# A decoder layer on one core: the context's values of four heads in one run of matmuls, with changes to loads, stores and the last norm

## The chip, the core and the metric

The kernel runs on one core of a Trainium2 chip. The core has a matmul engine (TensorE, PE in the profile; PEld is its loading of the stationary operand), VectorE (DVE), ScalarE (ACT), GpSimd (POOL), and SyncE (SP), which here only issues DMAs. Matmuls write to PSUM, eight banks of 512 fp32 columns for 128 partitions; the other operands lie in SBUF. Each engine works through its own queue in order, and semaphores tie the queues together. The metric is the device time of one execution in microseconds.

## The reference

One decoder layer with three sublayers, each followed by a residual sum and a layer norm. `x` has 8 sequences of 100 tokens and 1024 features, the context 8 sequences of 722 tokens.

```python
# 1: gated retention, 8 heads (128 for q and k, 256 for v)
o = rms(((rope(x@Wq)*scale) @ rope(x@Wk).T * D) @ (x@Wv)) * silu(x@Wg);  x = layernorm(x + o@Wo)
# 2: attention over the context and the own tokens: 16 query heads, 4 key/value heads of 128
q, k, v = rope(rms_norm(x@wq)), rope(rms_norm(x@wk)), x@wv
k = concat([rms_norm(ctx@wk_ctx), k]);  v = concat([ctx@wv_ctx, v])     # 722 + 100 rows, per sequence
x = layernorm(x + softmax(q@k.T*scale + mask) @ v @ wo)                 # each k/v head serves 4 query heads
# 3: feed-forward, 1024 -> 4096 -> 1024
x = layernorm(x + (silu(x@w_gate.T) * (x@w_up.T)) @ w_down.T)
```

## The kernel before

Activations lie features first: [128, 8 blocks, 400 tokens], in two halves of four sequences (`N` = 400). Every large product is made of three matmuls: an operand is split into a high part (a cast to fp32r on ACT) and a low part (the rest, a subtraction on DVE), and `mm3` adds high x high, high x low and low x high into one PSUM bank (L90, L93, L94; with them all products share these three lines). `split` and `split2` (L63 to L68) make the parts.

The order of the stages is retention with its output projection (`out_proj`, L238), the projections of queries, own keys and own values ("l2", L729), the attention loop (L773), the second output projection, the feed-forward, and the last norm (`norm_last`, L1099). `x` after a norm goes to DRAM (`zd`, `zd2`) and comes back in `out_proj` as `rs` (L264), two buffers, to be added as residual.

The context's weights: `core(h)` of the retention (L538) also splits one of the eight blocks of `wc` for each head (keys and values of the four heads in turn) and stores it to `wcd` (L561 to L566): SP stores the high part and its negative, and a DMA of GpSimd adds the raw weight to the latter, so that the low part is left. It is loaded ready-made later by `load_ws`, into tag `w`, which has four buffers of 1 MB.

The attention loop goes over 8 sequences ("batches", `b`) and 4 key/value heads (`kv`). For each batch, `load_context` brings the context in two parts of 362 and 360 tokens (`SH`, `SN`), in eight loads of two feature blocks each, and splits it into `cz`: the four buffers of the pool `big`, so only one batch's context is there. For each head:

- `context_keys` (L693): two projections of 24 matmuls (weights stationary, 362 or 360 context columns moving) into PSUM tag "a" (three banks); squares and a sum over partitions on POOL (L706), keys to `kall` (two buffers); the sums go by DRAM (`row`, then `rr`) from a row into columns and become the scale `rk` (L798 to L809). The first two heads of batch 0 are made during "l2" (`early`).
- `context_values` (L713): the same with the values' weights; the result, features first, is copied to `cvt`, turned by six transposes on PE (L794) into tokens first, and split into `vall` (two tiles, used in turn; seven chunks of 128 tokens by 128 features, the last ones partly own tokens loaded from `vd`).
- scores (L817): seven chunks, each 3 matmuls of 400 columns (four query heads x 100 tokens; 216 for the chunk of own tokens only), into tag "s" (four banks), evicted to `s` (one buffer) by DVE (L824) and ACT (L828); running maximum on DVE (L829), its reduction over partitions on POOL; subtraction, exponential, split into `ph` and `pl`, sum (L836 to L851).
- the products with `vall` (L854 to L859) in the order of chunks 5, 6, 0, 1, 2, 3, 4, into the one bank of tag "v"; the quotient, and the store to `o2d`.

The order of instructions on each engine is not written by hand: a planner takes the program and its own costs, and at each point puts next what is ready and stands first in program order; a buffer goes to whichever tile is written next. Work for later heads therefore runs ahead as far as buffers allow. `pin` and `issue_after` fix the order in a few places, and `pin`ned in `norm_last` are the subtractions `less(i)`, each over a pair of feature blocks.

Memory of pools is stacked: `y2` (the second output projection's `y` and `rs`, opened before the attention's pools, L764) has its own place beside them, and a tile of a later pool can lie where a tile of a closed pool lay and then waits for its last use.

Of the kernel before, what the change touches and what calls it, by code (L numbers as in the profile page):

```python
# [8 lines left out]
F32 = mybir.dt.float32  # L9
# [7 lines left out]
P = 128  # L17
# [5 lines left out]
SC, SH = 722, 362  # L23
# [17 lines left out]
def decoder_layer(ctx, tc, xT, cT, w1, wo1, w2, wo2, wc, w3, wd, gw, qw, kw, trig, dec, mask, out):  # L41
# [15 lines left out]
    def f32(ap):  # L57
        return ap.bitcast(F32)
# [23 lines left out]
    def load_ws(i):  # L82
        w = wp.tile([P, 2, KT * P], FR, tag="w", name="w", bufs=4)
        nc.sync.dma_start(out=f32(w), in_=f32(wcd[i]))
        return w
# [91 lines left out]
    wcd = dr.tile([2 * NKV, P, 2, KT * P], FR, name="wcd")  # L177
# [60 lines left out]
    def out_proj(half, w, load_o, res, yp, ybufs, p, make_z, dst, z, steps={}):  # L238
# [7 lines left out]
        for ms in [range(first)] + [[m] for m in range(first, KT)]:  # L246
# [15 lines left out]
            for m, acc in zip(ms, accs):  # L262
                rs = yp.tile([P, N], F32, tag="rs", name="rs", bufs=2)
                nc.sync.dma_start(out=rs, in_=res[half, :, m])  # L264
# [63 lines left out]
    def scaled(y, r, dst, z=None, behind=None):  # L328
        cast = None
        for m in range(KT):  # L330
# [6 lines left out]
            nc.sync.dma_start(out=dst(m), in_=y[:, m])  # L337
# [139 lines left out]
    with sbuf("l1", 2) as p:  # L477
# [60 lines left out]
        def core(h):  # L538
# [26 lines left out]
            nc.sync.dma_start(out=f32(wcd[h]), in_=f32(w))  # L565
            nc.gpsimd.dma_start(out=f32(wcd[h])[:, 1], in_=st, accum_op=ALU.add)  # L566
# [126 lines left out]
    def context_keys(kv):  # L693

        kall = ka.tile([P, 2, SC + T], FR, tag="kall", name="kall")
        wk = load_ws(2 * kv)
# [16 lines left out]
    def context_values(kv):  # L713

        wv = load_ws(2 * kv + 1)
        vt = ka.tile([P, SC], F32, bufs=1, tag="cvt", name="cvt")
        for hf in range(2):
            copy = nc.scalar.copy if hf == 0 else nc.vector.tensor_copy
            copy(vt[:, hf * SH:hf * SH + SN[hf]], proj(wv, cz[hf], SN[hf]))
        return vt  # L720
# [5 lines left out]
    for kv in range(NKV):  # L726
        groups += [[(kv, i) for i in range(2)], [(kv, i) for i in range(2, 5)]]
# [36 lines left out]
    y2pool = sbuf("y2", 1)  # L764
    y2p = y2pool.__enter__()
    with sbuf("cx", 2) as p, sbuf("c1", 1) as p1:

        ph = p1.tile([P, NC, N], FR, name="ph")
        pl = p1.tile([P, NC, N], FR, name="pl")
        valls = [p1.tile([P, NC, 2, P], FR, name=f"vall{i}") for i in range(2)]  # L770
        for t in [ph[:, 0], pl[:, 0]] + [v[:, 6] for v in valls]:
            nc.gpsimd.memset(f32(t), 0.0)
        for b in range(B):  # L773
            if b > 0:
                load_context(b)
            for kv in range(NKV):
                if early:
                    kall, row = early.pop(0)
                else:
                    step, (kall, row) = context_keys(kv)  # L780
# [3 lines left out]
                vall = valls[kv % 2]  # L784
                nc.sync.dma_start(out=f32(vall[C5:P, 5]), in_=f32(vd[kv, 0:P - C5, b]))
                nc.sync.dma_start(out=f32(vall[0:R6, 6]), in_=f32(vd[kv, P - C5:T, b]))
# [3 lines left out]
                vt = context_values(kv)  # L790
# [476 lines left out]
```

## Time and profile before

| | us |
|---|---|
| median of 3 runs (2482.09 to 2486.21) | 2483.2 |
| the profiled execution's own time | 2485.66 |
| its span in the profile | 2483.9 |
| PE busy | 2459.2 |
| DVE busy | 1953.3 |
| ACT busy | 1340.1 |
| POOL busy | 460.2 |
| from 920 to 1600 us (attention): DVE, ACT, POOL busy of 680 | 622.6, 414.7, 254.8 |

A page line such as "PE 2459.2 (99%) x14068" is busy time, share of the span and count of instructions. The slices cut the span into 40 equal parts of 62 us; a digit is the busy share in tenths. In the windows view each line has a stretch, its length, then busy time and count for PE, PEld, DVE, ACT and POOL, the granted TensorE clock, the share of DMA and GB/s. In the timeline a line has start, duration, engine, source line, operation, output<-inputs, shapes and count, and in brackets the engine's idle time before it and what ended it. Matmuls overlap their neighbours in the records, so that their price is the distance of starts. In the chain a line has start, duration and what it was, followed back from the end of the program.

### The profile page before, as it was taken

To read this page: it belongs to the slowest core of one execution; us is meant where nothing else is said; L and a number is where in the kernel's file an instruction comes from. 1 tells how busy PE (TensorE), PEld (TensorE's weight loads), DVE (VectorE), ACT (ScalarE), POOL (GpSimd) and SP (SyncE) were. 2 spreads that over 40 slices of the span, in tenths; PEclk is the share of its full clock that TensorE was granted. 3 is DMA by queue.
4 is the path that set the end of the run, shared out by engine and by line. 5 is a ranking of instruction groups with operands and counts; after the bars stand their busy time and mean duration, and the time that the engine had idled before them with its cause. 6 is when DMAs were issued, how large, how long until landed. Compare 5 with 4: busy or idle time off the path is not lost.

```text
span 2483.9 us, 37221 instructions
## 1 busy us (share of the span) xinstructions
PE 2459.2 (99%) x14068; PEld 2440.1 (98%) x14068; DVE 1953.3 (79%) x3101; ACT 1340.1 (54%) x2258; POOL 460.2 (19%) x234
## 2 busy tenths in 40 slices
PE   9999999999999999999999999999999999999997
PEld 9999999999999999999999999999999999999997
DVE  7777877566898698998998999748978777666756
ACT  6667676334888465666566656534545445432221
POOL 0111111000565333443443433100000000000000
PEclk9999999999999999999999999999999999999999
DMA  7333445775544555455555454565445444389731
GB/s 244 112 111 129 134 141 185 247 261 181 164 161 157 182 175 168 144 181 159 160 174 159 152 181 168 165 241 178 154 174 194 163 161 161 121 301 324 267 103 54
DMA packets 224451, 433.98 MB, mean 175 GB/s; under 512 B 47338, under 2 KB 168042, under 8 KB 211854
## 3 DMA queue, kind: packets, MB, share of 16 engines
q1 hardware_dynamic: 222542, 426.87, 51.2%
q0 software_dynamic: 1152, 4.19, 1.1%
q8 instruction: 111, 1.82, 0.3%
q14 instruction: 70, 0.57, 0.1%
q10 hardware_dynamic: 576, 0.52, 0.1%
HBM read 322.18 MB, written 109.35 MB: 174 GB/s over the span
## 4 chain that ended last, share of the span: by engine, by line
PE 93%; DVE 3%; DMA 2%; ACT 1%; issue 1%; SPq 0%; DVEq 0%; ACTq 0%
PE a L94 20%; PE a L93 20%; PE a L90 20%; PE s L94 9%; PE s L93 9%; PE s L90 9%; PE v L94 2%; PE v L90 2%; PE v L93 1%; PE s L554 1%; PE s L794 1%; PE s L166 1%; DVE y L331 0%; DMA cs<-in_cT 0%; DMA rs<-zd 0%
## 5 line engine op out<-in xcount | busy, mean ns | idle before, releaser
L90 PE MATMUL a<-big,w 128*128 128x400 f32 (+2 forms) x1808 | 609.8, 338 | 0.9 <-DVE y L424 0.7
L93 PE MATMUL a<-big,w 128*128 128x400 f32 (+2 forms) x1808 | 609.2, 337 | 0.2 <-DVE big L68 0.2
L94 PE MATMUL a<-big,w 128*128 128x400 f32 (+2 forms) x1808 | 608.0, 337 | 0.6 <-DVE w L68 0.6
L68 ACT CAST w<-wst 128x1024 fp32r<-128x1024 f32 (+1 forms) x231 | 239.6, 1039 | 386.2 <-PE s L94 146.0
L68 DVE TENSOR_TENSOR w<-wst,w 128x1024 fp32r<-128x1024 f32 (+1 forms) x231 | 280.6, 1215 | 135.0 <-ACT w L68 133.0
L90 PEld LDWEIGHTS a<-big,w 128*128 128x128 f32 x1808 | 340.0, 188 | 2.4 <-DVE y L424 1.0
L93 PEld LDWEIGHTS a<-big,w 128*128 128x128 f32 x1808 | 340.5, 188 | 1.6 <-DVE big L68 0.4
L94 PEld LDWEIGHTS a<-big,w 128*128 128x128 f32 x1808 | 340.7, 189 | 1.5 <-DVE w L68 0.9
L90 PE MATMUL a<-z,w 128*128 128x400 f32 x680 | 234.7, 345 | 0.4 <-ACT w L68 0.4
L93 PE MATMUL a<-z,w 128*128 128x400 f32 x680 | 234.7, 345 | 0.0
L94 PE MATMUL a<-z,w 128*128 128x400 f32 x680 | 234.5, 345 | 0.0
L90 PE MATMUL s<-big,w 128*128 128x400 f32 x664 | 230.0, 347 | 0.1
L94 PE MATMUL s<-big,w 128*128 128x400 f32 x664 | 228.9, 346 | 0.4 <-DVE w L68 0.4
L93 PE MATMUL s<-big,w 128*128 128x400 f32 x664 | 229.2, 345 | 0.0
L141 POOL PARTITION_ALL_REDUCE ss<-sq x56 | 148.4, 2651 | 325.8 <-DMA vd<-vs 185.6
L706 POOL PARTITION_ALL_REDUCE kss<-ksq x64 | 166.1, 2596 | 125.3 <-ACT ksq L705 124.6
L828 ACT ACTIVATE s<-s,rk 128x400 f32<-128x400 f32 x160 | 88.1, 591 | 101.1 <-DVE sm L848 66.7
L90 PEld LDWEIGHTS a<-z,w 128*128 128x128 f32 x680 | 127.6, 188 | 1.2 <-ACT w L68 0.8
L94 PEld LDWEIGHTS a<-z,w 128*128 128x128 f32 x680 | 128.4, 189 | 0.0
L93 PEld LDWEIGHTS a<-z,w 128*128 128x128 f32 x680 | 127.6, 188 | 0.4
L90 PEld LDWEIGHTS s<-big,w 128*128 128x128 f32 x664 | 124.6, 188 | 1.7 <-ACT w L68 0.4
L94 PEld LDWEIGHTS s<-big,w 128*128 128x128 f32 x664 | 125.1, 188 | 0.7 <-DVE w L68 0.7
(355 smaller groups left out, 5444.4 us busy)
## 6 DMA issues: line engine op xcount, KB each, us to landing
wst<-in_w SPq DMA_DIRECT2D x135, 512.0 KB
w<-wcd SPq DMA_DIRECT2D x64, 1024.0 KB
wst<-in_wo SPq DMA_DIRECT2D x64, 512.0 KB
hd<-h SPq DMA_DIRECT2D x12, 1400.0 KB
wst<-in_wd SPq DMA_DIRECT2D x64, 256.0 KB
big<-o1d SPq DMA_DIRECT2D x16, 800.0 KB
qd<-d SPq DMA_DIRECT2D x32, 400.0 KB
q<-qd SPq DMA_DIRECT2D x32, 400.0 KB
```

Source lines behind the costliest of these rows:

```text
L68: return nc.scalar.copy(hi, src), nc.vector.tensor_tensor(lo, src, f32(hi), ALU.subtract)
L90: i = nc.tensor.matmul(acc, lh, rh, start=start, stop=False, skip_group_check=chain)
L93: nc.tensor.matmul(acc, lh, rl, start=False, stop=False, skip_group_check=chain)
L94: nc.tensor.matmul(acc, ll, rh, start=False, stop=stop, skip_group_check=chain)
L141: nc.gpsimd.partition_all_reduce(y, x, P, op)
L166: nc.tensor.transpose(tr[0:T, b * P:(b + 1) * P], vt[:, b * T:(b + 1) * T], ident)
L554: nc.tensor.matmul(bt(o)[:, b], vv[:, b * P:(b + 1) * P], pf[:, b], start=True, stop=True)
L706: nc.gpsimd.partition_all_reduce(ss[:, at], sq[:, at], P, RED.add)
L794: nc.tensor.transpose(tr[0:rows, (c - c0) * P:(c - c0 + 1) * P], vt[:, c * P:c * P + rows], ident)
L828: nc.scalar.activation(sc, sp, AF.Copy, scale=rk[:, c:c + 1])
```

## The change

- The context is cut at 384 tokens in place of 362 (`SH`): three chunks of 128 lie in the first part, three (the last of 82) in the second.
- The values' weights of the four heads go to a tensor of their own, `wvd`, in which the four heads of one feature block lie side by side; the keys' weights stay in `wcd`. The DMAs are the same in number.
- `context_values` is called once for a batch, ahead of its heads. It loads four weight tiles (two feature blocks of all four heads each), and for each of six chunks of context tokens makes one product of 24 matmuls, in which the context's tokens are stationary (128, or 82 in the last chunk) and 512 columns, four heads x 128 features, are moving. The result is tokens first already, so there are no copies to `cvt` and no transposes; each chunk is split into `vall`, now one tile for all heads and batches.
- For head 0 of a batch the keys' weights get a tile of their own, `wk`, outside the four buffers of `w`.
- The first `s` tile is taken ahead of `ph`, `pl` and `vall`, and the pool `y2` is opened after the attention's pools.
- In "l2" the two groups of the last head change places: the one with its last two query heads and own keys comes before the one with its first two query heads.
- The loads of `rs` in `out_proj` (both projections) are issued by GpSimd.
- `norm_last` squares the mean's correction first, and then subtracts it from the pairs; its eight stores are issued by SP and ACT in turn.

```diff
@@ -20,7 +20,7 @@
 N = NB * T
 KT = D // P
 QT = KT // 2
-SC, SH = 722, 362
+SC, SH = 722, 384
 SN = [SH, SC - SH]
 NC = 7
 ORDER = (6, 5, 0, 1, 2, 3, 4)
@@ -79,9 +79,10 @@
             split(w, st)
         return w
 
-    def load_ws(i):
-        w = wp.tile([P, 2, KT * P], FR, tag="w", name="w", bufs=4)
-        nc.sync.dma_start(out=f32(w), in_=f32(wcd[i]))
+    def load_ws(src, w=None):
+        if w is None:
+            w = wp.tile([P, 2, KT * P], FR, tag="w", name="w", bufs=4)
+        nc.sync.dma_start(out=f32(w), in_=f32(src))
         return w
 
     pin = tc.keep_in_program_order
@@ -174,7 +175,8 @@
     o2d = dr.tile([B, P, NKV, 4, 2, T], FR, name="o2d")
     zd = dr.tile([2, P, KT, N], F32, name="zd")
     zd2 = dr.tile([2, P, KT, N], F32, name="zd2")
-    wcd = dr.tile([2 * NKV, P, 2, KT * P], FR, name="wcd")
+    wcd = dr.tile([NKV, P, 2, KT * P], FR, name="wcd")
+    wvd = dr.tile([P, 2, KT, NKV, P], FR, name="wvd")
     hd = dr.tile([QT - 1, 7, P, 2, QT, N], FR, name="hd")
     h3d = dr.tile([4, P, 2, QT, N], FR, name="h3d")
 
@@ -261,7 +263,7 @@
                 y = yp.tile([P, KT, N], F32, tag="y", name="y", bufs=ybufs)
             for m, acc in zip(ms, accs):
                 rs = yp.tile([P, N], F32, tag="rs", name="rs", bufs=2)
-                nc.sync.dma_start(out=rs, in_=res[half, :, m])
+                nc.gpsimd.dma_start(out=rs, in_=res[half, :, m])
                 if early:
                     nc.vector.tensor_tensor(rs, rs, early["mean"], ALU.subtract)
                     with tc.high_priority():
@@ -325,7 +327,7 @@
                 s2 = s3
         return s2
 
-    def scaled(y, r, dst, z=None, behind=None):
+    def scaled(y, r, dst, z=None, behind=None, turns=False):
         cast = None
         for m in range(KT):
             nc.vector.scalar_tensor_tensor(y[:, m], y[:, m], -0.5, r, ALU.mult, ALU.mult)
@@ -334,7 +336,7 @@
                     cast = split(z[m // QT][:, :, m % QT], y[:, m])[0]
             elif z is not None:
                 split(z[m // QT][:, :, m % QT], y[:, m])
-            nc.sync.dma_start(out=dst(m), in_=y[:, m])
+            (nc.scalar if turns and m % 2 else nc.sync).dma_start(out=dst(m), in_=y[:, m])
         return cast
 
     def norm_root(y, s1, p):
@@ -562,8 +564,14 @@
             st = load_raw(wc[h])
             nc.scalar.copy(w[:, 0], st)
             nc.scalar.activation(w[:, 1], f32(w[:, 0]), AF.Copy, scale=-1.0)
-            nc.sync.dma_start(out=f32(wcd[h]), in_=f32(w))
-            nc.gpsimd.dma_start(out=f32(wcd[h])[:, 1], in_=st, accum_op=ALU.add)
+            if h % 2 == 0:
+                to, wf, low = f32(wcd[h // 2]), f32(w), st
+            else:
+                to, wf = f32(wvd)[:, :, :, h // 2], f32(w).rearrange("p l (k n) -> p l k n", n=P)
+                low = st.rearrange("p (k n) -> p k n", n=P)
+            nc.sync.dma_start(out=to, in_=wf)
+            nc.gpsimd.dma_start(out=to[:, 1], in_=low, accum_op=ALU.add)
 
         def gated(h, g):
 
@@ -690,10 +698,10 @@
         for _ in context_steps(b, wp, 3):
             pass
 
-    def context_keys(kv):
+    def context_keys(kv, w=None):
 
         kall = ka.tile([P, 2, SC + T], FR, tag="kall", name="kall")
-        wk = load_ws(2 * kv)
+        wk = load_ws(wcd[kv], w)
         sq = ka.tile([P, SC], F32, tag="ksq", name="ksq", bufs=1)
         ss = ka.tile([P, 6 * P], F32, tag="kss", name="kss", bufs=1)
         row = dr.tile([6, P], F32, tag="row", name="row", bufs=2)
@@ -710,21 +718,25 @@
                 nc.sync.dma_start(out=row.rearrange("c p -> (c p)")[None, :], in_=ss[0:1])
         return step, (kall, row)
 
-    def context_values(kv):
-
-        wv = load_ws(2 * kv + 1)
-        vt = ka.tile([P, SC], F32, bufs=1, tag="cvt", name="cvt")
-        for hf in range(2):
-            copy = nc.scalar.copy if hf == 0 else nc.vector.tensor_copy
-            copy(vt[:, hf * SH:hf * SH + SN[hf]], proj(wv, cz[hf], SN[hf]))
-        return vt
+    def context_values(vall):
+
+        wv = [load_ws(wvd[:, :, 2 * j:2 * j + 2].rearrange("p l k v n -> p l (k v n)")) for j in range(QT)]
+        for c in range(NC - 1):
+            rows, hf, at = C5 if c == 5 else P, c // 3, c % 3 * P
+            acc = bank("a")[0:rows, :NKV * P]
+            for k in range(KT):
+                zh, zl = (cz[hf][k // QT][:, l, k % QT, at:at + rows] for l in range(2))
+                wh, wl = (wv[k // 2][:, l, k % 2 * NKV * P:(k % 2 + 1) * NKV * P] for l in range(2))
+                mm3(acc, zh, zl, wh, wl, k == 0, k == KT - 1)
+            split2(vall[0:rows, c, :, 0], vall[0:rows, c, :, 1], acc.rearrange("p (v d) -> p v d", d=P))
 
 
     early = []
     behind = list(behind)
     groups = [[(kv, 5) for kv in range(NKV)]]
     for kv in range(NKV):
-        groups += [[(kv, i) for i in range(2)], [(kv, i) for i in range(2, 5)]]
+        pair = [[(kv, i) for i in range(2)], [(kv, i) for i in range(2, 5)]]
+        groups += pair[::-1] if kv == NKV - 1 else pair
     unit = NKV
     with sbuf("l2", 2) as p:
         ctx0 = context_steps(0, p, 2, behind)
@@ -761,39 +773,32 @@
     z1pool.__exit__(None, None, None)
 
 
-    y2pool = sbuf("y2", 1)
-    y2p = y2pool.__enter__()
     with sbuf("cx", 2) as p, sbuf("c1", 1) as p1:
 
+        s = p1.tile([P, NC, N], F32, tag="s", name="s")
         ph = p1.tile([P, NC, N], FR, name="ph")
         pl = p1.tile([P, NC, N], FR, name="pl")
-        valls = [p1.tile([P, NC, 2, P], FR, name=f"vall{i}") for i in range(2)]
-        for t in [ph[:, 0], pl[:, 0]] + [v[:, 6] for v in valls]:
+        vall = p1.tile([P, NC, NKV, 2, P], FR, name="vall")
+        for t in [ph[:, 0], pl[:, 0], vall[:, 6]]:
             nc.gpsimd.memset(f32(t), 0.0)
         for b in range(B):
             if b > 0:
                 load_context(b)
+            context_values(vall)
             for kv in range(NKV):
                 if early:
                     kall, row = early.pop(0)
                 else:
-                    step, (kall, row) = context_keys(kv)
+                    w = p1.tile([P, 2, KT * P], FR, tag="wk", name="wk") if kv == 0 else None
+                    step, (kall, row) = context_keys(kv, w)
                     step(0)
                     step(1)
                 nc.sync.dma_start(out=f32(kall[:, :, SC:]), in_=f32(kd[kv, :, b]))
-                vall = valls[kv % 2]
-                nc.sync.dma_start(out=f32(vall[C5:P, 5]), in_=f32(vd[kv, 0:P - C5, b]))
-                nc.sync.dma_start(out=f32(vall[0:R6, 6]), in_=f32(vd[kv, P - C5:T, b]))
+                nc.sync.dma_start(out=f32(vall[C5:P, 5, kv]), in_=f32(vd[kv, 0:P - C5, b]))
+                nc.sync.dma_start(out=f32(vall[0:R6, 6, kv]), in_=f32(vd[kv, P - C5:T, b]))
                 q = p.tile([P, 4, 2, T], FR, tag="q", name="q")
                 nc.sync.dma_start(out=f32(q).rearrange("p h l t -> p h (l t)"),
                                   in_=f32(qd[kv, :, :, b]).rearrange("h p l t -> p h (l t)"))
-                vt = context_values(kv)
-                for c0, c1, rows in ((0, 3, P), (3, 5, P), (5, 6, C5)):
-                    tr = bank("s")
-                    for c in range(c0, c1):
-                        nc.tensor.transpose(tr[0:rows, (c - c0) * P:(c - c0 + 1) * P], vt[:, c * P:c * P + rows], ident)
-                    src = tr[0:rows, 0:(c1 - c0) * P].rearrange("p (c d) -> p c d", d=P)
-                    split2(vall[0:rows, c0:c1, 0], vall[0:rows, c0:c1, 1], src)
 
                 rr = p.tile([P, 6], F32, tag="rr", name="rr")
                 with nc.allow_non_contiguous_dma("a row turned into a column"):
@@ -808,7 +813,8 @@
                 nc.vector.scalar_tensor_tensor(rk[:, 0:5], r1[:, 0:5], 3.0, r0[:, 0:5], ALU.subtract, ALU.mult)
                 nc.vector.scalar_tensor_tensor(rk[0:C5, 5:6], r1[0:C5, 5:6], 3.0, r0[0:C5, 5:6], ALU.subtract, ALU.mult)
 
-                s = p1.tile([P, NC, N], F32, tag="s", name="s")
+                if b + kv > 0:
+                    s = p1.tile([P, NC, N], F32, tag="s", name="s")
                 mx = p.tile([P, N], F32, tag="mx", name="mx")
                 def part(ap, c):
                     ap = bt(ap)
@@ -855,7 +861,7 @@
                     c = ORDER[j]
                     n = N6 if c == 6 else N
                     o = bt(ov)[:, :, T6:] if c == 6 else bt(ov)
-                    mm3(o, vall[:, c, 0], vall[:, c, 1], bt(ph[:, j, :n]), bt(pl[:, j, :n]),
+                    mm3(o, vall[:, c, kv, 0], vall[:, c, kv, 1], bt(ph[:, j, :n]), bt(pl[:, j, :n]),
                         j == 1, j == NC - 1)
 
                 r = p.tile([P, N], F32, bufs=1, tag="r0", name="r0")
@@ -877,6 +883,8 @@
                 in_=f32(o2d[half * NB:(half + 1) * NB, :, g]).rearrange("b p h l t -> p b (h l t)"))
         return lambda k: (t[k // 4][:, :, k % 4, 0], t[k // 4][:, :, k % 4, 1])
 
+    y2pool = sbuf("y2", 1)
+    y2p = y2pool.__enter__()
     kapool.__exit__(None, None, None)
 
 
@@ -1141,14 +1149,13 @@
         summed(var, sqs[1][:, 0])
         summed(var, q7, stop=True)
         less = lambda i: pin(nc.vector.tensor_tensor(pair(i), pair(i), wide(delta), ALU.subtract))
-        less(0)
         vs = p.tile([P, N], F32, tag="vs", name="vs")
         nc.scalar.activation(vs, delta, AF.Square)
-        less(1)
+        less(0)
         pin(nc.vector.tensor_tensor(vs, var, vs, ALU.subtract))
-        less(2)
-        less(3)
-        scaled(y, inv_root(p, vs, eps_ln), dst)
+        for i in range(1, QT):
+            less(i)
+        scaled(y, inv_root(p, vs, eps_ln), dst, turns=True)
 
     for name in C:
         gated_block(0, name, None)
```

## The prediction

> **What bounds the kernel now.** The page comes first: TensorE (PE) against the other engines, then the busy slices.
>
> ```profile
> span 2483.9 us, 37221 instructions
> ...
> PE 2459.2 (99%) x14068; PEld 2440.1 (98%) x14068; DVE 1953.3 (79%) x3101; ACT 1340.1 (54%) x2258; POOL 460.2 (19%) x234
> ...
> DVE  7777877566898698998998999748978777666756
> ```
>
> PE sets the time: only work taken from PE, or a hole in it, moves the end. But in slices 14 to 26, the cross attention, DVE (VectorE) is at 80 to 90% or more. The windows view (PE, PEld, DVE, ACT, POOL busy, with counts; clock; DMA) gives one head, two batches of four heads, and the entry of the stage:
>
> ```profile
> 1103.80:1123.10 19.30, 19.30 (x121) 19.14 (x120) 18.72 (x39) 12.54 (x25) 6.82 (x4) 1.00 0.49 158
> 1123.10:1218.30 95.20, 95.20 (x578) 94.59 (x577) 87.92 (x155) 58.44 (x113) 37.34 (x21) 1.00 0.52 164
> 1218.30:1313.40 95.10, 95.10 (x578) 94.48 (x577) 87.92 (x154) 58.58 (x113) 38.03 (x21) 1.00 0.52 164
> ...
> 826.00:833.00 7.00, 4.11 (x25) 3.81 (x24) 0.21 (x1) 0.00 (x0) 0.00 (x0) 0.95 0.89 274
> 833.00:840.00 7.00, 6.78 (x23) 6.77 (x24) 4.34 (x10) 1.78 (x3) 0.00 (x0) 0.56 0.11 47
> ```
>
> PE has no hole in a batch of 95.1 us, because projections for later heads fill it while DVE does a softmax. In that head DVE was busy 18.72 of 19.30 us: a head cannot go much faster than this. The timeline of DVE marks head starts (first L824; here heads 3 and 0 of two batches), that of PE the prices of matmuls:
>
> ```profile
> 1103.76 0.37 DVE L824 SCALAR_TENSOR_TENSOR s<-s,msk 54x216 f32<-54x216 f32 x1
> 1123.14 0.36 DVE L824 SCALAR_TENSOR_TENSOR s<-s,msk 54x216 f32<-54x216 f32 x1
> ```
>
> ```profile
> 1011.30 0.35 PE L93 MATMUL s<-q,kall 128*128 128x400 f32 x1
> 1011.49 0.35 PE L94 MATMUL s<-q,kall 128*128 128x400 f32 x1
> 1011.67 0.49 PE L794 MATMUL s<-ident,cvt 128*128 128x128 f32 x3
> ```
>
> The durations overlap, so starts count. Over all pairs of equal shape in the trace the median from start to start is 183 ns with 400 columns, 165 with 360, 105 with 216, and 109 for a transpose.
>
> Last, what lies between a keys product and its first use (timeline of all engines), and three stalls (the chain that ended last):
>
> ```profile
> 846.57 0.47 ACT L705 ACTIVATE ksq<-a 128x360 f32<-128x360 f32 x1 [1.04 <-PE a L94]
> ...
> 854.58 0.30 ACT L802 ACTIVATE rr<-rr,eps_k 128x6 f32<-128x6 f32 x1 [1.45 <-DMA rr<-row]
> ...
> 856.41 0.15 DVE L809 SCALAR_TENSOR_TENSOR rk<-rr,rr 82x1 f32<-82x1 f32 x1
> ```
>
> ```profile
> 824.45 8.22 DMA kd<-d
> ...
> 1698.52 3.27 DMA rs<-zd
> ...
> 2470.81 0.51 ACT vs L1146
> ```
>
> **The values' matmuls.** Before, a batch takes 4 heads x 48 products of 362 or 360 columns, 192 x 0.1655 = 31.8 us, and 24 transposes x 0.109 = 2.6: 34.4. After, 6 chunks x 8 x 3 = 144 products of 512 columns. The line through 216 and 400 columns rises by 0.424 ns a column and gives 230 ns at 512, so 33.1: 1.3 less a batch, **-10.2** over eight. In proportion to the columns (183 x 512 / 400 = 234) it is -5.4, the other end.
>
> The Trainium skill (TensorE: Matmul & The Clock Gate, "Wait — 56ns, not 53.3ns?") gives the columns at 2.4 GHz plus about 2.5 ns, 216 ns at 512. That would make it -26, an estimate from the page; the trace's 183 at 400, where that rule says 169, speaks against it, and the sum goes by the trace.
>
> **What covered the softmax.** The removed products were the cover. After, a head leaves PE its keys (48 products, 8.0 us), scores and the products with the values (3.6 each): 15.2. DVE's head is 19.3 less the values' rows in it (vall 1.16, cvt 0.52), 17.6. So between two runs DVE is the bound, and PE must be fed by the next batch's run. There is one vall for all batches, so nothing of that run can leave PSUM before the last head has read its values; tag "a" has three banks, and by program order the run's first three chunks take them, ahead of the next keys. What follows release is serial. From head 0's start to the next batch's:
> - three heads x 17.6 and the eight context casts x 0.82 (median start to start on DVE): 59.4;
> - head 3's start to its first product with vall: 16.5 (1103.76 to 1120.30), less 1.7 of values' work; nine products until chunk 0 has been read, 1.4; cast and subtraction of the chunk, 1.2: 17.4;
> - chunks 3 to 5, 72 x 0.230 = 16.6, and twelve products left, 2.2: 18.8;
> - head 0's keys, lower in order: 8.0;
> - their sum of squares, its way over DRAM and the root, as in the rows above (846.57 to 856.46): 9.9.
>
> Sum 113.5, against PE's work of 33.1 + 4 x 15.2 = 93.9: 19.6 idle a batch. Lower end 0, if the keys come early (below). Upper end 22.7: the clock was granted at 0.56 for 7 us after the hole of 3.3 us at 830, which cost 3.1, and a longer hole would too. I take **16**: near the serial sum, whose links are rows of this stage, less 3.6, because the first and last links were timed with DVE nearly full. Seven boundaries are 112. In the last batch there is no further run: four heads take 70 us, PE has 45 of its own and about 18 of the output projection: 7. **+119**.
>
> **Scores' tile first, last group's order.** The first score's eviction waits for the kd store (8.22) whose tile lies under s; PE then stands 2.9 of 7 us and runs at 0.56 for 7 more: -2.9 - 3.1 = **-6.0**. If another late tile takes its place (vall, wk, or the four weight loads of the run behind the last group), 0.
>
> **Pool issues rs loads.** 32 loads leave SP. The hole they close: SP stands behind zd stores and weights, three rs loads come one after the other (4.25, 2.95, 3.27), PE waits 2.3 at 1700.6: **-2.3**. On POOL nothing else runs from 1606.9 on, so its queue is free; in the first projection it is idle too. As y2's memory now follows the attention's tiles, y and the first rs wait for its end; PE needs that only after a first group of about 65 us. If a load came late each time, 4.25 x 3 = +13.
>
> The rule that speaks against this part is in the Trainium skill (DMA: Bandwidth & Descriptors, "SWDGE vs HWDGE vs iDMA"): GpSimd writes a descriptor ring in SBUF, which DVE can lock it out of, and queues of SP and ACT have no such ring. No row here shows a delayed one; the eight Pool DMAs of before landed in 5.2 to 8.5 us.
>
> **Last norm, stores.** Today less(0) ends at 2470.78 and vs starts at 2470.81 on the same bank; with vs first the wait moves ahead of less(0), the four less still fill DVE, and L134 comes about 0.4 sooner. SP issues eight stores in 3.79 us beside eight L331 of 3.97; two queues save at most 0.4. Together **-0.5**, ends 0 and -0.8.
>
> **Stores of the values' weights.** Four of eight weights go out in 512 B runs. SP waited 62 us in seven waits (longest 11.5) for Pool's accumulation without a hole in PE there; that backlog hides it: 0. If each of four doubled its 6.2 on top: +25. Copies to cvt vanish from ACT and DVE; that is in the 17.6. Split 384/338 has the same columns: 0.
>
> **Sum** against the profiled execution (2485.7; its span 2483.9): -10.2 - 6.0 - 2.3 - 0.5 + 119 = 2585.7; it stood 2.5 above the median, so **2583**. Its own range: 10 a boundary (scale chain hidden) gives 2541, 22.7 gives 2630.
>
> **Rivals.**
> *The next keys come first.* wk has its own tile, so that they can. If they get a bank before the run's third chunk, scale and scores are ready when s is free, and the rest of the run lies beside the next softmax. DVE then needs 4 x 17.6 + 6.6 + 3 = 80, under PE's 93.9: idle 7 in all, 2485.7 - 19 + 7 - 2.5 = **2471**, up to 2485 with 2 a boundary. For it: PE had no hole in any batch of before, and there too keys ran ahead of transposes that had no bank. Against: these matmuls are later in program order than 144 ready ones. It decides below 19 us of new idle in all, 2.7 a boundary.
> *Stage one stalls on the short runs, and the keys do come first*: 2471 + 25 = **2496**. For it: SP's waits; against: no hole today.
> *The change does not do what it says*: the planner spreads the run over heads. With one vall it can't past chunk 2; that part is in the sum.
>
> **How the numbers follow.** Serial boundary 57 in 100, keys first 32, stage one 7, other 4. The measurement tells 0.2%, about 5 us. Of the keys' case four fifths lie under 2478: faster 0.28 (with some of the rest), same 0.07, slower 0.65. The range runs from 2468 to 2625 over both cases; the likeliest alone has 2541 to 2630.
>
> **What would show it.** PE idle of some 10 to 20 us a batch, with waits on evictions of vall or s and half clock after; head starts some 18 us apart inside a batch, 50 or more across batches; head 0's keys after chunk 5. If batches are 94 apart without holes, the keys came first and the forecast is wrong. The 512-column products should stand 230 apart, no hole at 830, no rs in the chain at 1690, the tail half a microsecond shorter.

## The result, and the profile after

The changed kernel takes 2664.8 us (median, 2664.0 to 2666.1), the kernel before 2484.7 in the same comparison: a ratio of 1.0728, 95% interval 1.0714 to 1.0741. The forecast was 2583 with a range of 2468 to 2625: the right side and the right mechanism, but 82 us short. The page of the changed kernel (lines as before: busy time by engine, then busy share and granted clock in 40 slices):

```profile
span 2663.8 us, 35955 instructions
...
PE 2495.3 (94%) x13492; PEld 2404.6 (90%) x13492; DVE 1933.2 (73%) x3021; ACT 1329.6 (50%) x2178; POOL 501.9 (19%) x265
...
PE   9999999999999797978879797989999999999998
...
DVE  6788776577985958668595857764888887766755
...
PEclk9999999999999898989899898989999999999999
```

The PE row of the kernel before, for comparison:

```profile
PE   9999999999999999999999999999999999999997
```

PE has 576 matmuls fewer (24 transposes and 48 products net per batch, times eight), yet is busy longer, and its row has dips in slices 14 to 27, where it had none. DVE was at 80 to 90% there; now its digits fall to 5. Both engines wait for one another.

Line numbers from here on are those of the kernel that is looked at; in the changed kernel `mm3` is L91, L94 and L95, and what was L824 is L830. The timeline of DVE in one batch of the changed kernel: L830 with 54x216 marks a head's first score (heads 1, 2, 3, then 0 and 1 of the next batch), `vall<-a` a chunk of the run leaving PSUM, L814 the scale of head 0; between them two lines of ACT, the squares of head 0's keys:

```profile
992.51 0.37 DVE L830 SCALAR_TENSOR_TENSOR s<-s,msk 54x216 f32<-54x216 f32 x1
...
1015.00 0.38 DVE L830 SCALAR_TENSOR_TENSOR s<-s,msk 54x216 f32<-54x216 f32 x1
...
1033.03 0.38 DVE L830 SCALAR_TENSOR_TENSOR s<-s,msk 54x216 f32<-54x216 f32 x1
...
1050.17 0.68 DVE L68 TENSOR_TENSOR vall<-a,vall 128x512 fp32r<-128x512 f32 x1
...
1051.85 0.36 DVE L830 SCALAR_TENSOR_TENSOR s<-s,msk 54x216 f32<-54x216 f32 x1
...
1069.41 0.69 DVE L68 TENSOR_TENSOR vall<-a,vall 82x512 fp32r<-82x512 f32 x1 [4.75 <-ACT vall L68]
```

```profile
1072.98 0.49 ACT L713 ACTIVATE ksq<-a 128x384 f32<-128x384 f32 x1 [3.60 <-PE a L95]
...
1076.66 0.45 ACT L713 ACTIVATE ksq<-a 128x338 f32<-128x338 f32 x1 [2.72 <-PE a L95]
```

```profile
1084.36 0.15 DVE L814 SCALAR_TENSOR_TENSOR rk<-rr,rr 82x1 f32<-82x1 f32 x1
...
1110.67 0.37 DVE L830 SCALAR_TENSOR_TENSOR s<-s,msk 54x216 f32<-54x216 f32 x1
```

From head 1 to head 1 it is 118.2 us where it was 95.1. The first three chunks wait for head 3's products with `vall` (1050.17); the other three (to 1070.1), head 0's keys (to 1077.1) and the scale (1084.5) follow one after the other, and head 1 starts 58.8 us after head 0. That is the chain the prediction wrote down. What it does to PE, in its waits and at one of the holes:

```profile
PE v L91 <- DVE sm L854: 115.0, 14, 9.9
PE a L91 <- DVE kall L716: 11.6, 7, 2.5
PE a L91 <- DVE y L272: 7.5, 1, 7.5
```

```profile
1036.57 0.27 PE L95 MATMUL s<-q,kall 128*54 128x216 f32 x1
1045.61 0.70 PE L91 MATMUL v<-ph,vall 128*128 128x400 f32 x1 [8.77 <-DVE sm L854]
1046.63 0.70 PE L94 MATMUL v<-pl,vall 128*128 128x400 f32 x1 [0.32 <-DVE pl L68]
...
1048.44 0.54 PE L94 MATMUL v<-pl,vall 128*128 128x400 f32 x1
1048.77 0.54 PE L95 MATMUL v<-ph,vall 128*128 128x400 f32 x1
```

Fourteen holes of 7 to 10 us, two in each of seven boundaries, before the products of heads 2 and 3: everything that PE may do is done, and the rest of the run has no bank. After each hole the products of 400 columns start 0.333 us apart, not 0.183, for 4 to 7 us. The windows view has the granted clock: 0.71 in the 33 us with the two holes of this batch, 0.91 over the batch, where it was 1.00 before:

```profile
1017.00:1050.00 33.00, 16.55 (x67) 14.97 (x66) 30.20 (x49) 18.83 (x31) 6.50 (x4) 0.71 0.19 59
992.50:1110.70 118.20, 99.99 (x505) 90.57 (x504) 83.83 (x144) 57.26 (x103) 40.67 (x21) 0.91 0.41 132
```

All of PE's time can be split by the distances between starts of neighbouring matmuls: the median for each number of columns, what exceeds it by over 0.4 us (a hole), and the rest (mostly the slow clock). Worked out so for the two traces (the stage's exit begins in the last batch; moving that border moves up to 3 us between two rows):

| us | before | after | difference | forecast |
|---|---|---|---|---|
| matmuls at their medians | 2446.4 | 2429.9 | -16.5 | -10.2 |
| entry of the stage (800 to 850), lost | 6.0 | 0 | -6 | -6.0 |
| attention, holes | 1.0 | 144.0 | +143 | +112, both |
| attention, slow pace | 1.5 | 37.5 | +36 | |
| exit and second output projection, lost | 7.6 | 29.8 | +22 | +7 - 2.3 |
| all else, lost | 7.1 | 8.9 | +2 | 0 |
| after PE's last product | 12.8 | 12.3 | -0.5 | -0.5 |

The sum is +180, the difference of the spans (2483.9 to 2663.8).

### The profile page after: what moved, and what is told of

Read it like the earlier page. It is cut to its first block, busy times and chain, and to the rows that moved or that the text cites. A ratio compares the mean times of both kernels' runs of the same rounds, so it can differ in the third digit from the quotient of the medians.

```text
span 2663.8 us, 35955 instructions
## 1 busy us (share of the span) xinstructions
PE 2495.3 (94%) x13492; PEld 2404.6 (90%) x13492; DVE 1933.2 (73%) x3021; ACT 1329.6 (50%) x2178; POOL 501.9 (19%) x265
## 4 chain that ended last, share of the span: by engine, by line
PE 74%; DVE 12%; issue 6%; DMA 5%; ACT 2%; POOL 1%; SPq 0%; DVEq 0%; POOLq 0%; ACTq 0%
PE a L95 16%; PE a L91 16%; PE a L94 16%; PE s L95 7%; PE s L91 7%; PE s L94 7%; DVE pl L68 2%; DVE s L849 2%; DVE sm L854 2%; DVE mx L835 1%; DMA cs<-in_cT 1%; PE v L94 1%; DMA rr<-row 1%; PE v L95 1%; PE s L556 1%
## 5 line engine op out<-in xcount | busy, mean ns | idle before, releaser
L91 PE MATMUL a<-big,w 128*128 128x400 f32 (+2 forms) x1184 | 403.8, 341 | 9.0 <-DVE y L272 7.5
L95 PE MATMUL a<-big,w 128*128 128x400 f32 (+2 forms) x1184 | 402.6, 340 | 0.4 <-DVE w L68 0.4
L94 PE MATMUL a<-big,w 128*128 128x400 f32 (+2 forms) x1184 | 402.2, 340 | 0.2 <-DVE big L68 0.2
L94 PE MATMUL a<-z,w 128*128 128x400 f32 x680 | 234.8, 345 | 0.0
L91 PE MATMUL a<-z,w 128*128 128x400 f32 x680 | 234.6, 345 | 0.0
L95 PE MATMUL a<-z,w 128*128 128x400 f32 x680 | 234.3, 345 | 0.0
L91 PEld LDWEIGHTS a<-big,w 128*128 128x128 f32 x1184 | 223.2, 189 | 11.7 <-DVE y L272 7.8
L91 PE MATMUL s<-big,w 128*128 128x400 f32 x664 | 230.0, 347 | 1.6 <-ACT w L68 1.1
L95 PE MATMUL s<-big,w 128*128 128x400 f32 x664 | 228.7, 346 | 0.4 <-DVE w L68 0.4
L94 PE MATMUL s<-big,w 128*128 128x400 f32 x664 | 228.9, 345 | 0.0
L95 PEld LDWEIGHTS a<-big,w 128*128 128x128 f32 x1184 | 223.5, 189 | 0.9 <-DVE w L68 0.9
L94 PEld LDWEIGHTS a<-big,w 128*128 128x128 f32 x1184 | 223.2, 188 | 0.9 <-DVE big L68 0.4
L714 POOL PARTITION_ALL_REDUCE kss<-ksq x64 | 174.2, 2722 | 212.0 <-ACT ksq L713 211.9
L91 PE MATMUL v<-ph,vall 128*128 128x400 f32 (+1 forms) x224 | 91.6, 409 | 117.8 <-DVE sm L854 115.0
L91 PEld LDWEIGHTS v<-ph,vall 128*128 128x128 f32 x224 | 53.6, 239 | 123.2 <-ACT ph L68 122.8
L91 PE MATMUL a<-w,big 128*128 128x512 f32 (+1 forms) x384 | 151.8, 395 | 13.1 <-DVE kall L716 11.6
L95 PE MATMUL a<-w,big 128*128 128x512 f32 (+1 forms) x384 | 150.5, 392 | 0.0
L94 PE MATMUL a<-w,big 128*128 128x512 f32 (+1 forms) x384 | 150.2, 391 | 0.0
L142 POOL PARTITION_ALL_REDUCE mb<-sm x32 | 86.4, 2700 | 271.9 <-DVE sm L854 260.3
```

The source lines that it names most:

```text
L91: i = nc.tensor.matmul(acc, lh, rh, start=start, stop=False, skip_group_check=chain)
L94: nc.tensor.matmul(acc, lh, rl, start=False, stop=False, skip_group_check=chain)
L95: nc.tensor.matmul(acc, ll, rh, start=False, stop=stop, skip_group_check=chain)
L142: nc.gpsimd.partition_all_reduce(y, x, P, op)
L714: nc.gpsimd.partition_all_reduce(ss[:, at], sq[:, at], P, RED.add)
```

## The experiments

Times are medians; each ratio is to the kernel before, run beside it (2483.7 to 2486.1).

### Is it the order and the held banks?

Two kernels each take out one link, a third both. The keys of head 0 first:

```diff
+            for kv in range(1 if b > 0 else 0):
+                w = p1.tile([P, 2, KT * P], FR, tag="wk", name="wk") if kv == 0 else None
+                step, kept = context_keys(kv, w)
+                step(0)
+                step(1)
+                early.append(kept)
             context_values(vall)
...
```

> The changed kernel with one step of program order turned round: from the second batch on, the keys of head 0 are projected before the run of the values, not after it. Theory A (the prediction's: the run's chunks hold the three banks of tag a until head 3's products, and chunks 3 to 5, head 0's keys and the scale follow one after the other): keys (8.0 us) and scale chain (7.7) leave the chain, and part of the 8.7 by which head 0 was longer than a head; 16 to 21 of the 24.3 lost at each of seven boundaries come back: 2664.8 - 112 to - 147, 2518 to 2553, and head 0 of the next batch starts some 20 to 30 us after head 3 in place of 58.8. Theory B (PE has too little work of its own beside a softmax, in whatever order): 15 or more a batch stay lost, above 2600.

2594.0 us, 1.0446 (1.0429 to 1.0464): 71 us back, not the 112 to 147 of theory A: 41 above its range, and 6 under the bound of theory B. The trace decides between them: of the two holes a batch one is left, in head 3's softmax (windows view of a batch and of that softmax, then the line of the waits):

```profile
1043.00:1150.70 107.70, 97.46 (x510) 88.19 (x509) 88.40 (x144) 55.88 (x103) 41.44 (x21) 0.95 0.43 145
1024.20:1043.70 19.50, 10.53 (x44) 9.66 (x44) 18.18 (x30) 12.51 (x21) 5.37 (x3) 0.74 0.16 53
```

```profile
PE v L91 <- DVE sm L859: 57.6, 7, 8.3
```

Seven holes in place of fourteen. The keys now fill one softmax; the run's chunks 3 to 5 still have no bank in the other.

Three chunks in two tiles, so that chunks 0 to 2 leave PSUM at once (for room, `wk` goes, and the quotient is written in place):

```diff
-        vall = p1.tile([P, NC, NKV, 2, P], FR, name="vall")
+        vfirst = [p1.tile([P, 3, NKV, 2, P], FR, name=f"vfirst{i}") for i in range(2)]
+        vrest = p1.tile([P, NC - 3, NKV, 2, P], FR, name="vrest")
...
+            vall = lambda c: vfirst[b % 2][:, c] if c < 3 else vrest[:, c - 3]
             context_values(vall)
```

> The changed kernel with the first three of seven chunks of the values in two tiles used in turn, the rest in one; head 0's keys' weights in tag w (for room), the quotient written in place. Theory A: chunks 0 to 2 leave their banks at once, chunks 3 to 5 are made before the release and hold the banks instead, so 16.6 us leave each of seven boundaries: - 116, 2549; keys and scale of head 0 stay behind the release. Theory B: no gain, 2640 or more.

2589.0 us, 1.0424 (1.0408 to 1.0439). Also 76 back, 40 short of theory A, and one hole of 7.2 to 7.7 a batch, in head 3's softmax too: now chunks 3 to 5 hold the banks, and the keys are what cannot run. So 16.6 us of work moved ahead gave 11: the two holes do not add up by what is moved, each is filled or not. To see whether writing the quotient in place had cost something, the run was made again with room from elsewhere (the unused part of `ph`'s and `pl`'s first chunk):

> As the run with three chunks twice alone, with the quotient in its own tile and the room from ph and pl. Theory A: 16.6 us leave each of seven boundaries, 2549 (2540 to 2560); the quotient in place had hidden about 5 a batch. Theory C: 2585 to 2592.

2589.2 us, 1.0415 (1.0395 to 1.0434), the number of theory C: it had cost nothing.

Both edits together, first with the quotient in place, then with its own tile:

> The edits of the keys-first run and of the three-chunks-twice run together: head 0's keys ahead of the values' run, and the first three chunks in two tiles. Each alone left one hole of 7.4 to 8.4 us in head 3's softmax, where PE had run out of work that it was allowed to do: chunks 3 to 5 in the one, the keys in the other. Theory A (the held banks and what is queued behind them are the whole of it): together they leave no hole, and a batch comes to PE's own 93 to 96 us against 118.5: 2664.8 - 7 x 22 to 25, and the exit of the stage unchanged at some 22 over before: 2490 to 2511. Theory C (a head of at least 18 to 19 us on DVE, with 26 for head 0 beside keys, sets a floor of its own): 100 us a batch or more, above 2530.

2530.4 us, 1.0188 (1.0172 to 1.0203): 19 over theory A's range, at the bound of theory C.

> As the run with head 0's keys first and three chunks twice, but the quotient has its own tile again; the room comes from ph and pl, whose first chunk (54 rows, 216 columns) gets tiles of its own size. Theory A (held banks and the order behind them are the whole boundary; the rest in that run was the quotient in place, some 5 us a batch): 2530 - 25 to - 35 = 2495 to 2505, a batch of 93 to 95 us. Theory C (a floor from DVE's heads): 2525 to 2532, a batch of 98 to 99.

2528.4 us, 1.0178 (1.0163 to 1.0193). The holes in the softmaxes are gone; what is left in PE's waits is small and mixed, and the exit's 8 us:

```profile
PE a L91 <- DVE kall L716: 10.1, 8, 2.0
PE a L91 <- DVE y L272: 8.2, 1, 8.2
PE v L94 <- DVE pl L68: 7.6, 6, 1.7
```

```profile
1039.50:1135.40 95.90, 91.97 (x487) 82.91 (x487) 86.56 (x142) 54.49 (x100) 46.28 (x21) 1.00 0.47 151
1135.40:1234.60 99.20, 95.11 (x506) 86.22 (x506) 88.45 (x143) 55.07 (x102) 45.74 (x21) 1.00 0.49 157
```

The loss in the attention is 47.0 us where the changed kernel's is 181.5: the order and the held banks are three quarters of it. For the last quarter theory A blamed the quotient in place, and falls there; the number is theory C's (2525 to 2532, 98.5 us a batch on the mean of six). Its reason is not shown by that: DVE is busy 86.6 of 95.9 us (windows view above, two batches), and PE's 6.7 a batch go in many waits of 2 us and less, for DVE, ACT and loads. What sets them stays open. (The runs with more `rs` buffers below show that another order of instructions alone can cost an attention 30 us, so it may be that.)

One more bank for the run:

```diff
-    banks = {"a": 3, "s": 4, "v": 1}
+    banks = {"a": 4, "s": 3, "v": 1}
```

> The changed kernel with four PSUM banks for tag a and three for tag s. Theory A: a fourth chunk of the run is made before the release, so 5.5 us (24 products x 0.230) leave each of seven boundaries: - 39, 2626; a loss from three score banks would come on top of it. Theory B (the order does not matter): no gain, 2660 or more.

2689.4 us, 1.0829 (1.0813 to 1.0846): slower than the changed kernel by 25, which by the time alone is theory B. But two effects work against each other here. The chain did get shorter where it should: head 3's start to the scale of head 0 took 46.5 us, not 51.4. But from that scale to head 1 it took 31.4 us, not 26.3, and the three heads after it 64.7 where they took 59.3; PE waited 28.6 us in 16 waits for ACT to empty a score bank. Bank for bank, the scores needed it more.

Scores of head 0 before the keys of heads 1 and 2:

```diff
-                    mm3(bt(sp), kh, kl, q[:, :, 0, t0:], q[:, :, 1, t0:], True, True)
+                    with tc.high_priority() if kv == 0 else nullcontext(): mm3(bt(sp), kh, kl, q[:, :, 0, t0:], q[:, :, 1, t0:], True, True)
```

> The changed kernel with the score matmuls of head 0 of each batch given high priority, so that keys of heads 1 and 2 no longer stand between them on PE. Theory A1: head 0 of a batch takes 26.3 us from its scale to the next head's start, against 17.6 of a head, because its last three scores are queued behind those keys; what PE then does later falls into the holes before heads 2 and 3: 5 to 8.7 back at seven boundaries, 2604 to 2630. Theory A2: head 0 is late for its scale and for work on DVE, ACT and POOL that comes with the keys, whatever PE's order: 2655 to 2675.

2659.0 us, 1.0709 (1.0694 to 1.0724). Theory A2: from scale to head 1 it is still 25.9 us. In that stretch of the changed kernel DVE, ACT and POOL also do the evictions and squares of heads 1 to 3's keys and half of the next context's casts, and wait for one another; which of these makes head 0 long was not tried alone.

Two heads to a run, in two tiles in turn:

```diff
-        wv = [load_ws(wvd[:, :, 2 * j:2 * j + 2]...) for j in range(QT)]
+        wv = [load_ws(wvd[pr, :, :, QT * j:QT * j + QT]...) for j in range(2)]
...
-            acc = bank("a")[0:rows, :NKV * P]
+            acc = bank("a")[0:rows, :2 * P]
...
+                vall = valls[kv // 2]
+                if kv % 2 == 0:
+                    context_values(vall, kv // 2)
```

> The changed kernel with runs of two heads (256 columns) in two tiles used in turn, in place of one run of four heads in one tile; head 0's keys' weights again in tag w. Memory, the other parts and the rest are as in the changed kernel. Theory A: a pair's tile is free while the other pair is in its softmax, so that no boundary waits: holes before the products of heads 2 and 3 gone. The run of a batch is 288 products of 256 columns at 0.122 us from the line through 216 and 400 columns, 35.1 against 34.4 before: + 5.6 over eight batches, so 2484.7 + 5.6 - 6 (scores' tile) + about 8 (exit of the stage, where y2's memory is now late) = 2492, 2480 to 2505. Theory B (the turning, copies and single heads were the cover, and any run loses it): over 2600.

2512.1 us, 1.0114 (1.0099 to 1.0129); 7 over the range of theory A, 88 under theory B. The values still come in a run without turning, PE is full, and a batch takes 97.3 us on the mean of six (windows view of one):

```profile
1025.90:1124.10 98.20, 97.40 (x656) 95.69 (x655) 90.21 (x148) 55.35 (x108) 41.12 (x21) 1.00 0.49 159
```

So a run without turning and copies need not lose the cover of the softmax, as long as there is a run for another tile to be done. (The kernel also halves the length of a run; that alone, with one tile, was not tried.) It gains nothing, since 288 products of 256 columns (0.120 us each, 34.6) cost what 192 at 362 or 360 and the transposes did.

### The exit and the small parts

The pool `y2` opened after the attention, alone on the kernel before:

```diff
-    y2pool = sbuf("y2", 1)
-    y2p = y2pool.__enter__()
     with sbuf("cx", 2) as p, sbuf("c1", 1) as p1:
...
+    y2pool = sbuf("y2", 1)
+    y2p = y2pool.__enter__()
     kapool.__exit__(None, None, None)
```

> The kernel before with one edit: the pool y2 is opened after the attention's pools, as in the changed kernel. The prediction gave this nothing (a first group of 65 us covers it). In the changed kernel and in the one with pairs of heads PE has a hole of 7.6 to 7.9 us where the first y waits for memory of the attention, with half clock behind it. Theory M (y2's place is the cause): + 8 to + 19, 2493 to 2504. Theory N (it is the last batch's short work, and not the place): within 2 us of before.

2496.6 us, 1.0054 (1.0042 to 1.0067): theory M. From head 0 of the last batch to PE's last product it is 984.8 us against 967.5, 17.3 more, with one hole where the first `y` waits (timeline of PE):

```profile
1594.16 0.35 PE L94 MATMUL v<-ph,vall 128*128 128x400 f32 x1
1605.22 0.70 PE L90 MATMUL a<-big,w 128*128 128x400 f32 x1 [10.70 <-DVE y L270]
```

The time rose by only 12, because the hole at 830 is gone too: nothing is lost there though `s` is taken in its old place. On the kernel before, either this edit alone or the small parts below (the scores' tile first, with the order of the last two groups) are enough for that hole; the two small parts were not taken apart.

All small parts on the kernel before, with the `rs` loads by Pool and by SP (diffs as in the change):

> The kernel before with all parts of the change but the run of the values (and what belongs to it: the cut at 384, wvd, wk, one vall, y2's place): scores' tile first, the order of the last two groups, rs loads by Pool, the last norm's order and stores. The prediction's terms: - 6.0 - 2.3 - 0.5 = - 8.8, 2475.7. The trace of the changed kernel, where the hole at 830 is gone, the one at the residual loads is 3.5 in place of 2.3, and the tail 0.5 shorter: - 5.5, 2479. If the small parts cost anything, 2485 or more, and the run is not the only cause.

> As the run of the small parts on the kernel before, but with the rs loads issued by SP as before. The difference of the two is the price of the loads by Pool. The prediction: 2.3 slower than with Pool's loads, 2478. By the changed kernel's trace: equal or up to 1.5 faster than with Pool's loads, 2477 to 2479.

2482.7 us, 0.9998 (0.9989 to 1.0007), and 2480.1 us, 0.9986 (0.9977 to 0.9995). Both profiled spans are 2477.6, 6.3 under that of before, since the hole at 830 is gone in both; the medians move by only 1.5 and 4.0, less than the 5.5 to 8.8 expected. (The profiled execution with Pool's loads was the fastest of its eleven, 3.2 under their median, so the medians are the better measure; what takes the rest back stays open.) Pool's loads bring nothing that can be told: the two intervals overlap. Their line in POOL's waits names a cause:

```profile
POOL rs L264 <- DVE y L270: 216.0, 25, 55.1
```

The loads wait for the two buffers that the additions free, not for a place in a queue; the runs with four buffers below bear it out. PE's hole there is 3.5 us with Pool, 2.6 with SP.

### What would beat both kernels

The small parts with loads by SP, and the cut at 384:

```diff
-SC, SH = 722, 362
+SC, SH = 722, 384
```

> The kernel before with the scores' tile first, the order of the last two groups, the last norm's order and stores (the run with loads by SP), and the context cut at 384 and 338 tokens in place of 362 and 360, its values still turned head by head. The prediction gave the cut nothing, since the columns are the same. In the traces a pair of products at 384 and 338 columns takes 173.5 + 153.5 = 327 ns from start to start, one at 362 and 360 takes 331: 1536 pairs of keys and values by 4 ns are - 6.1, 2474 against 2480.1. If the distance belongs to the other neighbours of those products and not to the cut, 2480.

2477.9 us, 0.9975 (0.9966 to 0.9984): faster than both kernels, and the best version here (a run below with the same parts and an unused tile, 2477.6, is equal to it). In its trace products of 384 and 338 columns stand 174 and 154 ns apart, 328 in place of 331 for a pair: 4.6 us for 1536 pairs. The median fell by 2.3 against the run before, between the two expectations, and the intervals of the two ratios overlap: the trace shows the cut's gain, the time does not.

Four buffers `rs` in the second output projection, by SP and by Pool, and again with the room taken from `ph` and `pl`:

```diff
-                rs = yp.tile([P, N], F32, tag="rs", name="rs", bufs=2)
+                rs = yp.tile([P, N], F32, tag="rs", name="rs", bufs=2 if ybufs == 2 else 4)
...
-                r.append(y2p.tile([P, N], F32, tag="rs", name="rs", bufs=2))
+                r.append(y2p.tile([P, N], F32, tag="rs", name="rs", bufs=4))
```

> The kernel of the run with the cut at 384 (small parts, loads by SP), with four buffers rs in place of two in the second output projection, and, for room, the attention's quotient written in place. Theory R (the loads of the residual are late because they wait for the two buffers that the additions free, as the waits of the Pool's loads say: 64.4 us until the additions; the issuing engine is not the limit): four rows are there when the additions begin at 1680, and of the hole of 2.9 us and the slow clock behind it (2.0) 2 to 4 go: 2474 to 2476 against 2477.9. Theory Q (SP's queue is the limit, as the prediction had it): the hole stays, 2477 to 2479.

> As the run with four buffers rs, but with the loads issued by Pool. Theory R: with buffers enough the issuing engine does not matter, within 1.5 us of that run. Theory Q: Pool's loads take 2 to 3 off it.

> The kernel of the run with the cut at 384, with four buffers rs and loads by SP; the quotient in its own tile, the room from ph and pl. In the run with the quotient in place the hole at the residual loads (2.9 us) was gone, but the attention was 31 us longer. If the edit of the quotient did that: 2473 to 2475 against 2477.9. If the rs buffers or their place did it: 2500 or more.

2508.1, 2510.7 and 2508.4 us (1.0098, 1.0106 and 1.0090, each within 0.0018; the difference between SP and Pool lies inside that). The hole at the residual loads is gone in the trace of all three, so theory R is right about it, though the times of both theories were missed. For the attention is longer: from head 0 of batch 1 to head 0 of batch 7 it is 600.5 us with four buffers (597.9 with Pool's loads) against 569.5. An unused tile in the place of the two buffers, and three buffers:

```diff
+    nc.gpsimd.memset(y2p.tile([P, 2, N], F32, name="pad"), 0.0)
```

> The run with four buffers rs (quotient in its own tile, room from ph and pl), but with two buffers and an unused tile of the size of the other two beside them. If the place does it: the attention is as long as with four buffers, and the hole at the residual loads is back: 2508 to 2513. If the buffers do it: as the run with the cut at 384, 2476 to 2480.

> The kernel of the run with the cut at 384, with three buffers rs in place of two, nothing else. If the place does it, a shift by 1600 bytes a partition may or may not: 2475 to 2477 where the attention keeps its order, 2500 or more where it does not. If the number of buffers does it, half of the 30 us: 2490 to 2495.

2477.6 us, 0.9976 (0.9966 to 0.9986), and 2506.8 us, 1.0090 (1.0073 to 1.0107). So with four buffers it is the buffers and not the place, since an unused tile of the same size costs nothing. Three buffers cost as much as four, where half was expected of the buffers; 2500 or more was the sign of the place there, and an unused tile of one buffer's size was not tried, so for three the place is not excluded. The heads already start at other times in batch 0, and each batch then repeats a hole of some 2 us and the slow clock behind it (PE's waits with four buffers by SP; the run with the cut at 384 has no such hole):

```profile
PE a L90 <- DVE kall L708: 11.2, 7, 1.9
```

That the planner settles into another order, because one more load is ready at the stage's entry, is argued and not shown.

## Why the prediction was wrong

**The mechanism held.** "There is one vall for all batches", three chunks in the three banks, then chunks 3 to 5, head 0's keys and the scale in a row: every link stands in the timeline, and the runs with keys first and chunks twice take three quarters of the loss away where it said; the last quarter is open. The rival "the next keys come first" did not happen by itself; made to happen, it gave 2594 and not 2471, because the keys alone fill one of two holes. The rival's "idle 7 in all" had no place for the softmax in which chunks 3 to 5 still lack a bank.

**The step that failed is "I take 16": the heads' link in its sum was too short, and the "less 3.6" had no row of its own.** Seven boundaries lost 179 us, 25.6 each: 20.4 in holes and 5.1 in slow pace. The links, forecast and measured in one batch:

| link | forecast | measured |
|---|---|---|
| heads 0 to 2 (scale of head 0 to start of head 3) with casts | 59.4 | 66.6 |
| to the first chunk's eviction | 17.4 | 17.8 |
| chunks 3 to 5 | 18.8 | 19.3 |
| head 0's keys | 8.0 | 7.0 |
| scale | 9.9 | 7.4 |
| sum, and PE's own work | 113.5, 93.9 | 118.1, 92.7 |

The discount expected shorter first and last links, on the ground that DVE would be less full. The last one was shorter, by 2.5 (the row it was read from ends at 856.56, 0.1 later than written). The first was longer, by 7.2: its heads took 26, 22.5 and 18 us, forecast as 17.6 each and 6.6 for the casts. Head 0 has the keys' evictions and half of the casts beside it on DVE, ACT and POOL. So of the 9.6 by which 16 fell short, nearly all is told: 3.6 are the discount, 4.6 the longer links and 1.2 PE's own work, which was less. Seven times 9.6 are 67 of the 82 us. Even the upper end, 22.7, was too low. The slow clock, which the prediction added there as 3.1, is no term beside the links but stands inside them: the nine products after release took 3.5 us at the slow rate and with a short wait (the first starts at 1045.61, the ninth at 1048.77), forecast as 1.4. In PE's account it is 5.1 of the 25.6.

**"In the last batch ... 7" and y2's move at nothing** gave +7 for the exit; with the residual loads it lost 22 more than before. The run with `y2` late alone shows 17.3 of it. "PE needs that only after a first group of about 65 us" overlooked that in the kernel before this group ran inside the last batch, its four additions too; that cover is gone when `y` has no memory before the attention ends.

**The small terms.** The values' products came at 227 ns, not 230, and the new cut, put at nothing, takes 3 to 4 ns off a pair: -16.5 with the keys' part, not -10.2. The Trainium skill (TensorE: Matmul & The Clock Gate, "Wait — 56ns, not 53.3ns?") would have 216; the trace decides for the higher one. The -6 for the scores' tile with the last group's order and the tail's -0.5 are in the trace of the changed kernel. Pool's loads -2.3 were not: the hole grew to 3.5. Its cause was read as SP's queue, where it was two buffers. The short stores of the values' weights cost 2 us at most: up to 800 us PE loses 6.5 us, 4.4 before.

## What to carry over

When a long product replaces many short ones, ask first where its results can go while the consumer is still busy: banks that wait for one tile stop all that comes behind them, and here a second tile (two heads at a time) was worth more than the cheaper product. Add up a serial chain at full length, with the engines' other work beside each link; a discount needs a row of its own. A load that comes late waited here for its buffer, not for the engine that issues it, and a tile that loses its early place loses the work that ran ahead into it. A buffer or two more made a whole stage 30 us longer here: look there too before a difference of that size is put down to an edit's own purpose.

## What was not expected of the hardware

- After the holes of 7 to 10 us the 400-column products stood 333 ns apart for 4 to 7 us, then 183 again. It is the half rate after idle time that the Trainium skill states (TensorE: Matmul & The Clock Gate, "What's actually happening"); in PE's account here it was 5 us a boundary.
- 384 and 338 columns stood 174 and 154 ns apart, 362 and 360 stood 166 and 165: the pair is 3 to 4 ns shorter for the same 722 columns.
- Two more buffers of 1600 bytes a partition, for loads that nobody waits for during the attention, made the attention 31 us longer; unused memory of the same size did not. That is a change in the program's order and not a trait shown of the chip; its cause is open.
